# A state-space layer's sum over states: products with the unit matrix, or turned blocks added up in PSUM

## The chip, the core and the metric

The kernel runs on one core of a Trainium2 chip, in float32 throughout. The core's engines run side by side, each through its own queue in order: PE (TensorE, products, with its weight loads shown as PEld), DVE (VectorE), ACT (ScalarE, functions and copies), POOL (GpSimd) and SP, which here only issues DMAs. [...] The metric is the device time of one execution in microseconds, as the median of several runs; fewer is better.

## The reference, cut to what matters

Two transformer-like layers run over 4 sequences of 1024 tokens with 128 channels. Layer 0 is a selective state-space block (256 inner channels, 16 states) followed by a mixture of 8 experts and a shared one; layer 1 is a differential attention followed by routed attention and experts. The change lies in the state-space block:

```python
def step(h, inp):
    u_t, d_t, b_t, c_t = inp
    dA = jnp.exp(d_t[:, :, None] * A)
    h = dA * h + (d_t * u_t)[:, :, None] * b_t[:, None, :]
    y_t = jnp.einsum('bdn,bn->bd', h, c_t)      # the sum over the 16 states
    return (h, y_t)
...
y = ys.transpose(1, 0, 2) + uc * D
y = y * jax.nn.silu(z)
return y @ W_out.T
```

So for each channel and token, 16 products `h * c` are added up, `uc * D` is added, the result is gated by `silu(z)` and goes through the output product.

## The kernel before

**Tiling.** Layer 0 works on eight half-sequences of 512 tokens (`Half`, g = 0 to 7). Channels lie on the 128 partitions, in two groups (j = 0, 1), tokens along the free axis, so that one state of one channel group is a 128x512 tile.

**One state of one group** goes through four steps. `decay` (L446, ACT) makes the exponential `m_da`. `drive` (L450, POOL) makes `m_hb` = du * b, in one of seven buffers. `scan` (L458, DVE) runs the recurrence over the 512 tokens into the PSUM tile `m_hh`; in the first half of a sequence L462 keeps the last column as state, and L463 multiplies by c back into `m_hb`. `summed` (L466, PE) adds `m_hb` to the group's sum in PSUM, by a product with the unit matrix `ident` as weights and `m_hb` as the 512 moving columns. The two sums live in `banks[0]` and `banks[1]` (`d_x` in the profile), two PSUM tiles that all halves use in turn. A float32 product of 512 columns is two PE instructions with two weight loads in the profile.

**Around it.** `front` makes the inputs of a half (products L310, L318, L330, L345). `between` takes over after the last state: L368 (DVE) adds the sum bank to `uc * D`, L371 gates, L377 is the output product; then layer norm, the routing of tokens to experts and the turned input `f_xnT`. `Experts` runs nine experts for a half: `up` (L478, PE), `gelu` (L485, ACT), `down` (L500, PE) and `weighted` (L511 on DVE, L512 on POOL). Small PSUM results of `front`, `between`, `end` and `up` share four rotating banks (`bank()`, `l` in the profile); `f_yp` and `m_hh` have one bank each.

**Order.** Nothing is scheduled at run time. The string `ORDER` was written by a planner: each letter emits one step, and every engine's queue has its instructions in that order. For layer 0, `F` is a step of `front`, `f` fetches b and c of a state by two DMAs on SP, `a`, `r`, `s`, `y` are decay, drive, scan and summed, `B` and `E` are steps of `between` and `end`, and `u`, `g`, `d`, `w` are up, gelu, down and weighted. Halves overlap: while one half is scanned, PE and ACT run the experts of an earlier one. Exponentials and gelus use different function tables of ACT; each change from one to the other puts a table load (ACT_TABLE_LOAD) into ACT's queue.

In layer 1, the attention turns 128x128 blocks of its weights by PE (`nc.tensor.transpose`, L846) and copies them out of PSUM on ACT (L851).

Of the kernel before, what the change touches and what calls it, by code (L numbers as in the profile page):

```python
# [10 lines left out]
F32 = mybir.dt.float32  # L11
# [6 lines left out]
P = 128  # L18
# [28 lines left out]
def model_kernel(ctx: ExitStack, tc: tile.TileContext, a: dict, out: bass.AP):  # L47
# [100 lines left out]
    def normalized(dst, w, n, pool):  # L148
# [9 lines left out]

    TAKES = "GHIJKNOQ"
    ORDER = (  # L160
        "FFFFFFFFFFFFFFFFfFfFFFaFraFffFrsraafffaFafaaysaysrfyasrayasrrrryFFrssFyFayrrsFrrafrssaraFsFyfsyayysy"
        "fssFasaFayyaFFayfrFrysfrarsyrsyrsrrrsfyaFaaFsrfFyyssfyrrasrsayassryasaysaayayfrarsyfyyysaFrrssyfrFFB"
        "rBFaaBFsrfBrFsrFByFyFfBFrysfBsBaBBaayBrfuuuBrusBaBrFggfsguauyByaggaryaaasysrFsryrrsfBFdyudfgasyruruy"
        "wgggsuygfssasduaaarudrguryugfyuaysguyusgrFwfyrsauaagsrsrgdaydguFgfrdrufrywguysgraFsssayrgrryysfufugf"
        "usyuuagsgdryaaysruuayayusyswfaygdfadrargsyusuFgggBBBygaaaBayfrrraasruwdgrsgdBayFrsyFdywFsdBaruuFfrsf"
        "wsgBByyffBrsyruygdusFrBaasyffrgyrgsdauBauysayrasuBruadygswgdsrrugBgsuagrrysayFrfayFuBBuswagysgFysryg"
        "frusBayfaasuradFsaddswuayfsdarugugfugysrgugyFgufgFraursssayyrFsryryauaEgywuufdggadryaauEfssyagygEuru"
        "sggrBwruuFfrsugyrygarddasyudafgBrrwugyafBgudggFsysuBugrydudgsgwBBFugyuFBFwrFfgBrassudfsaraFsBFFfdwrg"
        "ysrsfrasuyaBBrFrugyagyauaaysayugdfrsysugydgausrrFawfyayBsarsFBFrudysFasrafauaygBdruFFyugfswysygsgrfy"
        "gBsFasBduurdsrafEyurudadFfyFsggwugEgwEyuudyFFrfgrsudafaaugwyguyasryyussyusdggggBaardBguaBuaauywrdudg"  # L170
        "fygBaufssuyadrBgfrsgurgwrFrusadBrsryagrgBFygrFuysBBuFgfrywsgugdBarryusffayBaafssssyararFyFrBsydurFug"
        "guBgyswgrauayBFfasyysyusaBFsdfuggByruradyuafrFsgggdusufyfdguraugasuywrdFgswdsFrgFuygrryrFaasfayruysa"
        "auragwFyusrydudgrgsFugafyfugursyFwugdgrduagyFsfsrausaayygfgdadwruursrBayfuyasgBFgagduwgaFsFadFgarasB"
        "ssufryyyrdrwauuysFguggBryasarsdauFBsygguwsFfusfgadsByydrrFyyfygsuysfyrsuarFsFEBrggyurdBFwfBgfarBfdyu"
        "usraaEfgsuadwsaEBafBusBdBryuygyrrrwrugugggyusagygBBFarrFdysuasduuauwygydsfgsfFuussFufurggrduurgaugyy"
        "dgauFfdwarasyuygsugyugsdyggaagygrusrwraaaudasuagggasBBrsyuawBsryrgfrBaBufrgrrrgFdsfayfrBFyuyadFuyasu"
        "frrdgggBfswusyFFFEsgugayduyBudsssawfyBEgsduygBasBrrdudrwfaufrsyuyuEgafFBuuasuryagguyggayaaFrggBgrrsd"
        "BarysrrawssysrdawyufgysyBFBgdFdusrwrsusayuyfudyuaFgdfrgrusggFuggfrwsduygFasagrdsuysayyuugggaaEadwysf"
        "uuyEuygsyrsgEduBawuuugBBggrgBddyfruaurBdggarwdauudgrufsgywuasyBrsgfrBruBygBgdBafufBsuggfduwysByaBugu"
        "gsugrdugasyuyrsBruaywagduggadrsyugrBsffruwragryrugaaausfraBagyyugdsrsrgsfuasuyryradsyusddagsuyswsguf"  # L180
        "gayudfsadgwgaurwugduggrsryguyayssryudurafyyuraggssywyayEygsgdayasrgyuEsuugrgysydBguBBwgduBEgduguBduw"
        "guBguggdudLSBBBSBdguuuwuggSdSSSwguSBguggduupBBpgppBugpgquuuBugqpBgdduqwpdgudwguggguuquwdpgdpgudqguwu"
        "ugqpduwguddwuggugugddugpugugdgdqwuguuduggEgqduggpgpwdEwqEdqwppqEEqppEqqRPMMXPMXMXcXPMcMCXXPMMcCXCTPX"
        "MMcXPXTMXTTMCXPTcMXTTMcPXMCCMTXTTPXcTMMVXPXccCMMCTXVTXPMTCXTcMCTPXMcVMCXTPMXTXcTMXTCPMXcMTXVPMTcXMCC"
        "TTXPMcTMVXTXPMMTCXcCpqTPXTMXcMVXTPTMcpXTqCMCXPTMXcMCVXPMTcpXMCTqPXMcMTXTXTPTCMcXpqTMXCPMTMcXVTPXCMMc"
        "TXVXPMcTCXTpMPpCqMMXXTqcXPCTMMXVTcPMXTMVXTcPCMXTCXMcTTPXMTMVXXcTcPMMCTCXVXTPTMXcMTpqPCMXCTXMVTPXMTcc"
        "XpqCMTXPTMMCXXVTPTMXcTMpCqPcMXTMXVTPXTCMcXMTXpPcMcMCqXTVPXMTMXpqCTcPMXTCXcCTTPCMXMXTMcpPCMqpXcMTVXTP"
        "MXcTCMXVTPXpTMcMXVTCXPMTTcCXTMTPXCMpXTcMXVPMcTXTMTCCPXMcMTXCXVTPTMXTTPcMXCMcTXMVPMXTXCcTTPMCXMXTMXVP"
        "TpcpMXMcCqPMqXTMXVCXTcPTMTMXpqcpPCXMcqVXTMTPCXTTppMMXcPCCqqXTMXcMCVTPMMXTcpCXqXpPqMXcVTTCMPXMTMXcTTC"
        "PXTMcMCXVTPXTMpXTcMCPqXMTcXCMVTPMXTcXMpTCqPMXTMcVXTPXMTCTXMpcTPCqMXcMTXVTPXMMCTXTpqcCXkPMcXVTTPMXMTM"  # L190
        "TcXpCCTPqMXcTXVMTPMMVCkXXXlkcPMXcCTpMPMqVkXXPMMlXcTMTcXkCCTlXPTTMXcTTCMXPTMklXCTMTXcPTMCMXVPkpcMXqMV"
        "XTTXCPcTMCTcXMpqTPkCXMclTXTMVXPTTMXpMckqlXCCPMcMTXXVTPMTpXMqklXPcMTXCMVCTPXMcTTpMcXXqklcPCMMTVCXXPTc"
        "TMCTpMkCXqPXlTMkkcXlMPlXTMXMXCVcTPMTMXVTCTPcXTMkMclXklXPTMTkXpPMlCCXcMCqMTXXVTPTccTMkXlMCpCPqXMTXMVT"
        "cTXPCTMMXcVXTPTCklpMMXcqTPCMXMTcXXVTPcTTMpMkCXqPXlCTMMcVXXTcPMTCTXklpMPMqMXTVcXCXTPTMTMkpXclPXMCMqCT"
        "XVTXPMTXcMklcXkPTlMMCcCXTCTPXTMMTkXlXkcPMcVMCVXTPXTMCXcMkTTXkPMMVcXXCTPTMcCCTXTPMMXkXkcMCTTPMXXMTcVk"
        "PMXcTCTMXTTXPMMXcVXpTpPMCTcXMVCXTPTTMMpXTcpPpCMCqXVqXTMTXcPTpMXMCqpcPMqCMXTXVTPXTMcMcpXpCPqqMMXTVXCX"
        "TcPTTMXppqCPMXcqTMcCMXCTXVPMTMXVTcCXPTMcMTXTpqXPTMCTXpcMTqXCPTMXcMVTPXTMTMXcCCpTPqXMcTMXkVPXTMpXMCcT"
        "PqCMXcTXMVTXPMMcTXCTCpPMqXcMTXVTPMXTCTMpXPkqMMcXXclkVPMCXTVXMTPkCXMXMcTlXPcMCTTMXkTPlXTcklMMCXcTCTPM"
        "XTTMCcXXVcPMkTCCXVMTTPXMTTcXTpMPqkMCXMcCplVXqXPMTTXklpMPcMqVXXMTCTPMcXTcTMXpkqCPlMXTMXVTCXPMTMXccpqk"
        "XPlCTMMXVTXcPCTpMkqlMcXTCTPMMXTCVXTXPcTMXcMCklklPXMCTTTMcVXTPXMCTMkXklPclMXTXMVTPCMXTpcXCMkPlqcMXTXM"  # L200
        "XVCTPTTckMXplMSPqCXTcMMCTVXPMXcTMVXTXPTMMTkCcXclTCXPTpqMMpkXSqXPMlCTTcXMCVPMXTcMcTkXpPlqXTTMMCcCVXSP"
        "MXkXclpPCMMCqXTTXTcTMPMkXlXTMkcPlXMMTVXXTCPTCMcMTcXCTkPlXkMXMVkkkTCTPXMkTcMXcTXTPMXCMVCTPMcXTMCTXXcV"
        "PCMMTTcXTPXkMTMXcVTCXPMTcCMXVTPMXTCcXMCTpXcTPMTMTXVPXMTpTpMpXCqTPpcMXMqVXCTPXTMccMXpqCpPMMqXXcCTVCXP"
        "TTMMpXqpqcPMXTMVXTCPMcCXMcCTTpXpqPMXMcqTTXCVPMXcMkTTCpXTPMqXTcMXCVXTPTMXMcpCTqPXTMcXMVTPCXMTcTXTTMPX"
        "CMcCTXMVTPMXcTXppqMCPMXcqCVMXTTXPTMTcpXTMCPqMXMTVXTPMcXcTXpPkMqMMXlVXCckTPXMCCTXMcVPkMkXllMcXCTTXPTM"
        "MkclXTTPXMCMTXTTCcPCMXTMTVcXPMMVkXXpCqcTPXMTTXpTPMqckMXlCXMVCXTPMTTpXqcklMPcMMXTXCVXTCTPcTMXpkMPqXlc"
        "MMCCTXVTXPTMpMXkqclXPMCMcTXVTPXTCTMcTCpXMkPclqXTMMXVcXTCTPTkMXMkcPllCMCXTVXTTMXPcTMMXXkcklPTClMMXCVT"
        "cXPMTcpkXPMqCXlTMMTXTCTPXMTMTpckXPClcMqMXcVVXPXTTkMMXClpPqcXMMCTVXTTPCXTTMcpcMkXqlPMXTMVCXTXCPTMcpCM"
        "XklcPMMqCXTXVTPXMccMTpkXqPlXCMMTTXTTCcPXMMkclXkTPClMXTCMXTcTPMkXlXkMXVPCcMVXTMXcCTPTMXcMVPXMMTCTcCXT"
        "XTPMTXMTXCcTPMTcCCXTMXPMcVXTTMPXkMTpMXXTPqCMcMTXVcppPMXpqXVCTTMPCXMXkcMTVPcMXMXTVCPXTCMTXcCTcMTPXCMT"  # L210
        "XcMCTXVPTTMXTMTXPcCMTcMVCXTPMXTTMXcXCTTcPMCMXVXVcCTTTTkkTTVkVZk00kGkklkGllk0lkkG0lklG01kGlkkllkklkll"
        "klk0lklGklklklklklkl0kGl0kGkk0k10kGk0YG20H302GIIG03HG202IIG2G50G2I00GG0G00GG0I02IG0GGJ2I0J2IG200G2GI"
        "10I00HG1G2G2I2I0IH0G420G7I22IGI0223IJ12IG210I2IH0GI0GGH22II0G240I21GHI22II20IG20GI0G120H2I12G1I0HI21"
        "1IGH23220I1GHIHI2JHI12KI21IH2KH1I36H113JH2H1J1HI2H11344HI1JK22H1HHK3J133JH11IJ3HIH1HJ3113H3H11HH31JJ"
        "JJ3133JHJ43J3J3KJ36H1JHJ11H34HKJ3J14HKO11H3H1O6HJ3J33J1JH313JHJ433OJK1341JKJ3J4H474K363KJ34HJJO345J3"
        "KKNK3JJ4N36K4J4OK463K4K4K3O4JKJ643OKK44KK643J5O6JKO644KNK654O4KK6O4K6644NK6OO44KOO6OK6O66OKO64OK656O"
        "NO454KK6O6O4NK64OK66O6O6O5N4OK4K6O456N4K5OK6O66NO5O556NN6N6Q5OOO6QO576N65Q7QOON67N7O5Q5N56ON5NN5Q6N5"
        "N5O7QN655NON75Q77NQ5N575N7Q5N6N5QN77Q55N75QQNQ7QN7Q577QQ77Q7Q7Q74QQ7NKQ5N57QN7Q7Q75QN75NQ7557Q7QN7NQ"
        "5Q57NQO7NQ74Q5N75Q77NQQ757Q7NQKQ7Q7Q"
    )  # L220
    f1 = tc.alloc_tile_pool(name="f1", bufs=1, side="right")
    f2 = tc.alloc_tile_pool(name="f2", bufs=2, side="right")
    ph = ExitStack()
# [18 lines left out]
    def bank(shape=None):  # L242
        return ps.tile(shape or [P, HALF], F32, name="l0")
# [25 lines left out]
    class Half:  # L269
# [93 lines left out]

        def between(self):

            y = self.uc
            for j in range(2):
                nc.vector.scalar_tensor_tensor(  # L368
                    y[:, j, :], y[:, j, :], vec[:, j, V_D : V_D + 1], banks[j], ALU.mult, ALU.add
                )  # L370
            nc.vector.tensor_tensor(y, y, self.zs, ALU.mult)  # L371
            yield
            yield
            po = bank([P, 4, C])
            for i in range(4):
# [87 lines left out]
            nc.vector.tensor_tensor(hb, hh, self.ct[n], ALU.mult)  # L463

        def summed(self, n, j):
            nc.tensor.matmul(banks[j], ident, self.hb[n, j], start=n == 0, stop=n == NS - 1)  # L466

    class Experts:

# [983 lines left out]
```

## Time and profile before

| | |
|---|---|
| median of 3 runs | 2672.36 us (2665.95 to 2677.88) |
| the profiled execution: its time, its span | 2661.41 us, 2659.6 us |
| granted TensorE clock, mean | 0.967 |
| PE, DVE, ACT, POOL busy, share of the span | 91%, 80%, 73%, 45% |
| sums, L466 | 512 PE instructions, first at 44.6 us, last at 859.9 us |
| experts' products, L478 and L500 | 576 PE instructions each |
| first product of layer 1's attention, L811 | at 965.6 us |

The whole span is a mean over stages with different limits. Layer 0 takes the first 965 us or so, the attention of layer 1 runs to about 2050 us, the rest is the routed layer. A stage is read best from busy times in stretches: an engine that is busy for all of a stretch sets its length, and an engine that idles for a few us only is close behind. Lengths of PE instructions overlap[...]; what one costs is the time from its start to the start of the next.

### The profile page before, as it was taken

The page shows a single profiled execution, that of the slowest core. Times are in us where ns is not written, and L with a number is a line of the kernel's source. Part 1 is how long each engine was busy: PE and PEld are TensorE (multiplying, and loading weights), DVE is VectorE, ACT ScalarE, POOL GpSimd, SP SyncE. Part 2 cuts the span into 40 slices and gives each one's busy share as a digit, 9 for nine tenths or more (in the row PEclk, how much of TensorE's full clock was granted, in tenths as well). Part 3 has the DMA queues.
Part 4 walks back from the last instruction along what each step waited for, and adds up shares of the span by engine and source line. Part 5 has one row for each costly group of instructions (what it writes and reads, how often), then busy time and mean ns, then how long its engine had stood idle before and what let it go on. Part 6 is the DMA issues. An engine that isn't in the chain of part 4 may idle for free.

```text
span 2659.6 us, 32447 instructions
## 1 busy us (share of the span) xinstructions
PE 2423.0 (91%) x10886; PEld 1182.7 (44%) x10886; DVE 2140.0 (80%) x4086; ACT 1949.9 (73%) x3058; POOL 1209.1 (45%) x619
## 2 busy tenths in 40 slices
PE   5699999999999978989998999899988889998987
PEld 2244444444444434445454545454544444444442
DVE  5988998898887448898889889988897776777656
ACT  5398889999998648889988998999896234332423
POOL 4868767867656125555556555654553000000000
PEclk8799999999999989999999999999999899999999
DMA  6323334433343411102110211021100000000000
GB/s 184 105 89 107 105 90 105 103 105 88 97 99 76 134 58 33 45 5 80 40 41 1 80 40 40 2 75 39 39 9 1 1 0 5 5 4 5 0 1 16
DMA packets 84010, 143.07 MB, mean 54 GB/s; under 512 B 11634, under 2 KB 27395, under 8 KB 83843
## 3 DMA queue, kind: packets, MB, share of 16 engines
q1 hardware_dynamic: 82722, 140.14, 18.8%
q8 instruction: 86, 1.41, 0.2%
q10 hardware_dynamic: 1120, 0.86, 0.1%
q14 instruction: 82, 0.66, 0.1%
HBM read 121.29 MB, written 19.66 MB: 53 GB/s over the span
## 4 chain that ended last, share of the span: by engine, by line
PE 63%; DVE 16%; ACT 14%; issue 3%; POOL 3%; DMA 0%; ACTq 0%; DVEq 0%; POOLq 0%
PE f_yp L500 8%; PE l L478 8%; PE d_sp L811 7%; PE r_a L1089 6%; PE d_x L466 6%; ACT d_pt L825 6%; DVE d_m L821 6%; PE d_x L860 5%; PE d_x L846 4%; PE r_a L1239 2%; ACT d_wT L851 2%; DVE m_hh L458 2%; DVE d_pt L839 2%; PE r_b L1216 2%; PE r_b L1067 1%
## 5 line engine op out<-in xcount | busy, mean ns | idle before, releaser
L821 DVE TENSOR_REDUCE d_m<-d_sp 128x1 f32<-128x1024 f32 x512 | 612.1, 1218 | 95.3 <-PE d_sp L811 93.6
L825 ACT ACTIVATE d_pt<-d_sp,d_m 128x1024 f32<-128x1024 f32 x512 | 574.7, 1123 | 54.5 <-DVE d_m L821 42.1
L450 POOL TENSOR_TENSOR m_hb<-m_du,m_bt 128x512 f32<-128x512 f32 x256 | 456.2, 1804 | 139.4 <-PE d_x L466 124.5
L836 POOL TENSOR_TENSOR d_pt<-d_pt,d_cf 128x1024 f32<-128x1024 f32 x128 | 263.4, 2058 | 474.7 <-DVE d_cf L831 385.9
L811 PE MATMUL d_sp<-d_k,d_q 32*128 32x512 f32 x2048 | 299.4, 652 | 56.5 <-ACT d_pt L825 54.3
L846 PE MATMUL d_x<-ident,d_pt 128*128 128x128 f32 x2048 | 316.3, 285 | 28.8 <-ACT d_wT L851 11.4
L846 PEld LDWEIGHTS d_x<-ident,d_pt 128*128 128x128 f32 x2048 | 219.8, 142 | 262.3 <-issue 94.4
L851 ACT COPY d_wT<-d_x 128x512 f32<-128x512 f32 x512 | 291.7, 591 | 60.8 <-PE d_x L846 57.9
L837 POOL TENSOR_TENSOR d_pt<-d_pt,d_pt 128x1024 f32<-128x1024 f32 x128 | 315.6, 2466 | 10.0
L466 PE MATMUL d_x<-m_hb,ident 128*128 128x512 f32 x512 | 266.0, 624 | 34.8 <-DVE m_hb L463 34.4
L478 PE MATMUL l<-f_xnT,w 128*128 128x512 f32 x576 | 281.6, 594 | 3.1 <-ACT f_ht L485 2.1
L500 PE MATMUL f_yp<-f_ht,w 128*128 128x512 f32 x576 | 274.2, 605 | 5.6 <-DVE f_cb L511 3.8
L860 PE MATMUL d_x<-d_wT,d_v 128*64 128x256 f32 x2048 | 249.0, 386 | 3.0 <-ACT d_wT L851 2.4
L485 ACT ACTIVATE f_ht<-l,b 128x512 f32<-128x512 f32 x288 | 185.3, 687 | 67.6 <-PE l L478 53.8
L446 ACT ACTIVATE m_da<-m_delta,neg_a 128x512 f32<-128x512 f32 x256 | 171.7, 714 | 38.1 <-DVE m_hh L458 32.4
L512 POOL TENSOR_TENSOR f_acc<-f_acc,f_cb 128x512 f32<-128x512 f32 x64 | 115.1, 1799 | 163.8 <-DVE f_cb L511 163.7
L458 DVE TENSOR_TENSOR_SCAN m_hh<-m_da,m_state,m_hb 128x512 f32<-128x512 f32 x128 | 175.6, 1372 | 16.4 <-ACT m_da L446 3.7
L463 DVE TENSOR_TENSOR m_hb<-m_hh,m_ct 128x512 f32<-128x512 f32 x256 | 176.0, 688 | 7.5
L458 DVE TENSOR_TENSOR_SCAN m_hh<-m_da,m_hb 128x512 f32<-128x512 f32 x128 | 169.7, 1326 | 13.0 <-POOL m_hb L450 1.7
L860 PEld LDWEIGHTS d_x<-d_wT,d_v 128*64 128x64 f32 x2048 | 136.2, 137 | 94.6 <-issue 18.9
L466 PEld LDWEIGHTS d_x<-m_hb,ident 128*128 128x128 f32 x512 | 98.0, 199 | 171.7 <-issue 96.8
L500 PEld LDWEIGHTS f_yp<-f_ht,w 128*128 128x128 f32 x576 | 108.6, 192 | 145.8 <-issue 129.0
(277 smaller groups left out, 3599.9 us busy)
## 6 DMA issues: line engine op xcount, KB each, us to landing
m_bt<-m_bcd SPq DMA_DIRECT2D x128, 256.0 KB
m_ct<-m_bcd SPq DMA_DIRECT2D x128, 256.0 KB
f_cb<-f_cbd SPq DMA_DIRECT2D x64, 256.0 KB
d_q<-d_qf SPq DMA_DIRECT2D x128, 128.0 KB
d_qf<-d_qks SPq DMA_DIRECT2D x16, 512.0 KB
d_kf<-d_qks SPq DMA_DIRECT2D x16, 512.0 KB
d_k<-d_kf SPq DMA_DIRECT2D x128, 64.0 KB
x<-in_x_dram SPq DMA_DIRECT2D x4, 512.0 KB
```

Of the source, the lines that this page charges most:

```text
L450: nc.gpsimd.tensor_tensor(self.hb[n, j], self.du[:, j, :], self.bt[n], ALU.mult)
L458: nc.vector.tensor_tensor_scan(hh, self.da[n, j], hb, 0.0 if self.h == 0 else state[:, j, n : n + 1], ALU.mult, ALU.add)
L466: nc.tensor.matmul(banks[j], ident, self.hb[n, j], start=n == 0, stop=n == NS - 1)
L478: nc.tensor.matmul(self.hp[i], w1[:, e, k * P : (k + 1) * P], self.half.fT, start=True, stop=True)
L500: nc.tensor.matmul(self.yp[e][0], w2[:, e, k, :], ht[:, k % 2, :], start=k == 0 and e < E, stop=k == NK - 1)
L811: nc.tensor.matmul(self.sp[s][:, c * HALF : (c + 1) * HALF], q[g, self.qb * P : (self.qb + 1) * P], k[g, :], start=True, stop=True,)
L821: nc.vector.tensor_reduce(self.m[s], self.sp[s], AX.X, ALU.max, negate=True)
L825: nc.scalar.activation(pt, self.sp[s], AF.Exp, bias=self.m[s], accum_out=self.se[:, s : s + 1])
L837: nc.gpsimd.tensor_tensor(p, p, p_2, ALU.add)
L846: nc.tensor.transpose(tp[:, i, :], self.pe[0][:, kb * P : (kb + 1) * P], ident)
L851: nc.scalar.copy(wTs[key][:, :, a, qi * P : (qi + 1) * P], tp)
L860: nc.tensor.matmul(op[a * 64 : (a + 1) * 64, :], self.batch.v[hp][:, c * 4 + i, a * 64 : (a + 1) * 64], wTs[self.n // (2 * QG), c][:, i, a ...
```

## The change

`summed` no longer multiplies by the unit matrix. Each 128x512 tile `m_hb` is taken as four 128x128 blocks; each block is loaded as weights, the unit matrix moves through as 128 columns, and PE works in its mode for turning (`is_transpose`). The turned blocks are added to what the bank holds, so at the end a bank holds the sum with tokens on the partitions and channels along the free axis, block by block.

`between` has to turn it back: two copies on ACT bring the banks into SBUF (`yt`, in the two buffers of `f_xn`), eight plain turns on PE put them into two of the four rotating banks (`yp`), and the multiply-and-add of L368 reads those instead of the sum banks. This adds steps, so `B` stands 144 times in `ORDER` instead of 128 times, and the planner wrote a new `ORDER` for the whole kernel. Its other letters are as many as before.

```diff
     ORDER = (
-        "FFFFFFFFFFFFFFFFfFfFFFaFraFffFrsraafffaFafaaysaysrfyasrayasrrrryFFrssFyFayrrsFrrafrssaraFsFyfsyayysy"
+        "FFFFFFFFFFFFFFFFfFFFFFarFraafsfarfasfsfyrfyraaaarfaassfrraFsafyrysraarrssyyaaaFrsarssysFfyryaFyfrFfy"
...
         def between(self):
 
             y = self.uc
+            yt = [f2.tile([P, 4, C], F32, name="f_xn") for _ in range(2)]
             for j in range(2):
+                nc.scalar.copy(yt[j], banks[j].rearrange("p (n c) -> p n c", c=C))
+            yield
+            for j in range(2):
+                yp = bank()
+                for i in range(4):
+                    nc.tensor.transpose(yp[:, i * P : (i + 1) * P], yt[j][:, i, :], ident)
+                yield
                 nc.vector.scalar_tensor_tensor(
-                    y[:, j, :], y[:, j, :], vec[:, j, V_D : V_D + 1], banks[j], ALU.mult, ALU.add
+                    y[:, j, :], y[:, j, :], vec[:, j, V_D : V_D + 1], yp, ALU.mult, ALU.add
                 )
             nc.vector.tensor_tensor(y, y, self.zs, ALU.mult)
-            yield
             yield
...
         def summed(self, n, j):
-            nc.tensor.matmul(banks[j], ident, self.hb[n, j], start=n == 0, stop=n == NS - 1)
+
+            for i in range(4):
+                nc.tensor.matmul(
+                    banks[j][:, i * P : (i + 1) * P],
+                    self.hb[n, j][:, i * P : (i + 1) * P],
+                    ident,
+                    is_transpose=True,
+                    start=n == 0 and i == 0,
+                    stop=n == NS - 1,
+                    skip_group_check=True,
+                )
```

## The prediction

> **What bounds the kernel now.** First the page's busy times, then the first layer cut at the first scan of each of its eight half-sequences (columns: busy us and instructions of PE, PEld, DVE, ACT, POOL; granted clock; DMA share; GB/s):
>
> ```profile
> PE 2423.0 (91%) x10886; PEld 1182.7 (44%) x10886; DVE 2140.0 (80%) x4086; ACT 1949.9 (73%) x3058; POOL 1209.1 (45%) x619
> ...
> 41.50:124.80 83.30, 51.60 (x79) 15.52 (x79) 76.01 (x125) 40.37 (x55) 79.95 (x40) 0.75 0.38 106
> 124.80:219.10 94.30, 89.61 (x216) 38.69 (x216) 83.75 (x113) 83.12 (x104) 65.11 (x34) 0.94 0.32 96
> 219.10:317.80 98.70, 94.80 (x241) 42.12 (x241) 89.20 (x158) 84.97 (x108) 79.22 (x42) 0.98 0.38 108
> 317.80:430.10 112.30, 109.50 (x282) 49.14 (x281) 102.14 (x165) 95.30 (x120) 78.60 (x45) 0.98 0.34 93
> 430.10:535.10 105.00, 104.11 (x264) 46.33 (x263) 94.85 (x175) 99.80 (x121) 79.91 (x44) 1.00 0.39 104
> 535.10:640.10 105.00, 104.65 (x271) 47.13 (x270) 94.72 (x132) 100.02 (x124) 75.77 (x43) 0.98 0.36 99
> 640.10:750.70 110.60, 110.60 (x288) 50.18 (x287) 95.29 (x173) 101.67 (x126) 74.54 (x44) 1.00 0.39 100
> 750.70:858.20 107.50, 106.47 (x275) 48.46 (x274) 86.00 (x129) 99.58 (x121) 65.82 (x39) 1.00 0.37 87
> 858.20:965.60 107.40, 104.35 (x302) 49.72 (x300) 43.16 (x156) 57.06 (x83) 17.36 (x14) 1.00 0.39 110
> ```
>
> From half 1 on PE is the limit, 95 to 100% busy. But ACT is right behind: from half 4 on it idles 5.2, 5.0, 8.9 and 7.9 us. Half 0 is DVE's. The last row is the tail after the last scan, again PE's. A busy PE need not be at its peak, so I take PE's cost from starts, in the timeline (start, length):
>
> ```profile
> 310.84 1.02 PE L478 MATMUL l<-f_xnT,w 128*128 128x512 f32 x2
> 311.69 0.60 PE L429 MATMUL l<-ident,f_acc 128*128 128x128 f32 x4
> 312.13 1.02 PE L466 MATMUL d_x<-m_hb,ident 128*128 128x512 f32 x2
> 312.99 1.88 PE L478 MATMUL l<-f_xnT,w 128*128 128x512 f32 x4
> ```
>
> A product of 512 columns (two instructions) holds the queue from 312.13 to 312.99, 0.86 us; four turned blocks from 311.69 to 312.13, 0.44 us. Last, what DVE and ACT wait for between 60 and 860 us, and the groups that price the rest:
>
> ```profile
> DVE f_cb L511 <- PE f_yp L500: 20.0, 9, 5.0
> DVE o_st L250 <- PE l L377: 9.9, 5, 4.0
> ...
> ACT f_ht L485 <- PE l L478: 19.9, 25, 2.2
> ```
> ```profile
> L846 PE MATMUL d_x<-ident,d_pt 128*128 128x128 f32 x2048 | 316.3, 285 | 28.8 <-ACT d_wT L851 11.4 <-POOL d_pt L837 8.5 <-ACT r_lnc L792 2.0
> L851 ACT COPY d_wT<-d_x 128x512 f32<-128x512 f32 x512 | 291.7, 591 | 60.8 <-PE d_x L846 57.9
> L485 ACT ACT_TABLE_LOAD x100 | 128.3, 1283 | 2.1 <-PE l L478 0.3
> L446 ACT ACT_TABLE_LOAD x99 | 127.0, 1283 | 2.6 <-DVE m_hh L458 0.9
> ```
>
> DVE's waits in that stretch add up to 57 us, 33 of them for PE. Its idle time there is about 93 us; the other 36 us are steps of under 0.2 us between its own instructions, some 5 us a half, which nobody ends earlier.
>
> **The change part by part.**
>
> The sums (L466): 256 products at 0.86 become 256 groups of four turned blocks at 0.44: 256 x 0.42 = 107.5 us off PE.
>
> Turning back in `between`: 16 groups of four plain turns, 16 x 0.44 = +7.0 us on PE. PE's net is -100.5 us, about 12.5 a half in the steady part.
>
> [...] The group of plain turns at L846 has 285 ns for one. [...] But 285 ns is how long one is shown, not how far apart they start: the timeline has 0.11 us a block, and I use that. As for the clock: between 985 and 2050 us, where L846 turns 2048 blocks, 512 groups at 0.44 to 0.59 us (a quarter of the time), the granted clock is 0.99. In the new first layer turns take 32 x 0.44 = 14 us of a half's 105. I put no clock loss.
>
> Adding to what is in PSUM with a turned block is not in the trace. Ends: 0.44 us a group, as plain turns; or 0.89, if such a block costs as an ordinary product of 128 columns (L377: 16 instructions, two a block, in 1.78 us), which puts PE at 256 x 0.03 + 7 = +15 us. [...] I take 0.44: the same kind of instruction, and ordinary products that add (L478 starts afresh, L500 adds) step alike.
>
> Copies out of the two sum banks: 16 on ACT by L851's row, 16 x 0.591 = +9.5 us. Table loads: the built order of ACT has 250 in the first layer against 256, -6 x 1.283 = -7.7 us. ACT's net is +1.8 us, but not evenly spread: up to the first decay of half 7 it is about +8, after it -6. DVE is unchanged: the 16 L368 instructions read a PSUM bank before and after. POOL and SP have the same instructions and DMAs, in almost the same place against the scans; nothing of theirs is moved past a queue.
>
> The new wait: the copies stand in ACT's queue between gelus and decays, and each waits for the last of a half's sums. Behind it are the gelus that free PSUM banks for `up`, and the next half's first sum waits for the copy as it waited for L368. I take nothing for it: in the order 1 to 5 scans of the next half stand ahead of that first sum (2 to 4 before), at 1.35 + 0.69 us each, and seven m_hb buffers let scans go on. Without that cover it costs up to a few us a half (rival C).
>
> **The sum.** PE's 100 us can't all be had: what a half can shrink is set by the next engine. Half 0: DVE idles 7.3, less 5 of steps: 2 us. Halves 1 to 3: DVE's 10.6, 9.5, 10.2 less 5 each: 15 us (ACT has more). Halves 4 to 7: ACT's 5.2, 5.0, 8.9, 7.9 less some 1.3 of steps each: 22 us (DVE has as much or more). The ceiling is 39 us, 37 with ACT's 1.8. How much of it comes? As long as PE leads, it runs at 99%; in the second layer's attention (985 to 2050), where PE, DVE and ACT are near each other, PE is busy 971.7, DVE 935.2 and ACT 948.3 of 1065, so the fullest still idles 9%. After the change the first layer looks more like that. I take half: -18 us.
>
> The tail: the order puts 45 `up` and 27 `down` behind the last scan (44 and 27 before), so PE-bound work of about 107 us stays; the chain of copy, turn and L368 is longer by 1.2 + 0.9 us, beside leftover products of half 6. +1 us. The second layer's instructions are the same, with some neighbours swapped: 0, a few us either way.
>
> So -17 us on the profiled execution's own time, 2661.4 to 2644.4. It was 11 us below the median of the three runs (2672.36); I carry the difference over: 2655 us, -0.65%.
>
> **Rivals.**
>
> A, the forecast (0.52): ACT and DVE become the limit and return about half the ceiling. For: ACT at 95% in halves 4 and 5 already. Gain 10 to 28 us: 2644 to 2662.
>
> B (0.16): PE was what broke the others' flow, the ceiling is returned whole and shorter waits let the neighbours move too. For: 33 of DVE's 57 us of waits name PE, and gelu waits 19.9 us for L478. Against: the attention stage shows no engine reaching 97%. 37 to 46 us: about 2630.
>
> C (0.12), slower: the handing-over of the sum banks. The copy stands in the fullest queue; a late copy holds the next half's first sum, then m_hb fills, POOL's L450 stops (it waited 124.5 us for L466 in all before) and DVE's scans with it. Each handing-over that stalls 5 us costs 7 x 5 = 35 against the gain of 17: +18, about 2690. It decides from 2.5 us each on. Against: L368 stood in a queue nearly as full, and waited 2.2 us in all. The dear end of the adding turns (+15) lands at the same place.
>
> D (0.20): ACT is already the limit in disguise: its extra 8 us before half 7 eat what the halves from 4 on could give, and only halves 1 to 3 gain. 0 to 10 us: 2662 to 2672.
>
> **How the numbers follow.** A difference of 0.5% (13 us) is about what measurement can tell from none; the three runs span 12 us. Faster by more: all of B and 0.75 of A, 0.55. Slower by more: C and a little noise, 0.13. Within: 0.32. The range reaches from B's end, 2626, to C's weaker form, 2684.
>
> **What would show it.** Right: sums' groups step 0.44 us; PE's busy share in halves 4 to 7 drops to about 90%; ACT's rises to 97% or more; halves 4 to 7 last 102 to 106 us; the first attention product (965.6 us before) starts near 949; second layer unchanged. Wrong: groups of 0.8 us or more (adding turns are dear); ACT idle before or behind the copies, and POOL's waits for the sums growing (C); a granted clock under 0.95 in these halves; halves of under 100 us (B: ACT wasn't a floor).

## The result, and the profile after

The changed kernel takes 2645.99 us in the median (2645.25 to 2647.33), against 2675.12 us for the kernel before beside it (2665.95 to 2677.94): a ratio of 0.990 (0.987 to 0.992), 1.0% faster. Its profiled execution took 2645.31 us, with a span of 2643.5 us, 16.1 us less than the span before. The medians differ by 29 us and the traces by 16, since the traced execution of before (2661.41 us) lies at the fast end of that kernel's runs; what a longer one of them spends its time on was not traced. Line numbers have moved: `decay` is L453, `drive` L457, the scan L465, the multiply by c L470, the sum L475, `up` L495, `gelu` L502, `down` L517; in `between` the copies are L369, the turns L374, the multiply-and-add L376, the output product L384.

The busy times of the page, and the first layer cut at the first scan of each half and at the first attention product, as before (columns: busy us and instructions of PE, PEld, DVE, ACT, POOL; granted clock; DMA share; GB/s):

```profile
PE 2346.8 (89%) x11462; PEld 1213.8 (46%) x11462; DVE 2143.2 (81%) x4086; ACT 1950.2 (74%) x3068; POOL 1208.3 (46%) x619
```
```profile
42.10:126.40 84.30, 41.83 (x151) 26.66 (x152) 76.93 (x125) 44.43 (x58) 78.97 (x41) 0.62 0.37 104
126.40:222.60 96.20, 82.08 (x288) 44.35 (x289) 86.06 (x114) 82.75 (x103) 65.34 (x36) 0.91 0.31 99
222.60:326.00 103.40, 89.34 (x313) 46.19 (x312) 90.90 (x157) 96.18 (x118) 73.33 (x42) 0.92 0.32 99
326.00:437.20 111.20, 98.81 (x349) 51.14 (x347) 102.01 (x164) 99.78 (x125) 71.72 (x44) 0.95 0.32 98
437.20:543.00 105.80, 96.25 (x340) 48.97 (x339) 93.37 (x175) 97.26 (x123) 83.10 (x45) 0.98 0.32 98
543.00:641.20 98.20, 96.21 (x347) 49.44 (x346) 90.15 (x133) 95.48 (x122) 75.10 (x41) 1.00 0.38 106
641.20:743.60 102.40, 97.45 (x362) 51.18 (x361) 93.79 (x166) 97.04 (x122) 78.02 (x43) 1.00 0.36 106
743.60:839.50 95.90, 92.50 (x342) 49.01 (x341) 88.13 (x129) 89.38 (x114) 73.34 (x41) 1.00 0.32 99
839.50:948.80 109.30, 104.82 (x308) 50.87 (x306) 45.57 (x162) 59.23 (x87) 17.37 (x14) 0.99 0.40 119
```

Halves 0 to 4 together became 7 us longer (500.9 us against 493.6), halves 5 to 7 became 27 us shorter (296.5 against 323.1), the tail 2 us longer. The first attention product starts at 948.8 us instead of 965.6. From there to the end of the span it is 1694.7 us against 1694.0: the second layer is unchanged. (In the traces of all experiments this part takes 1693.8 to 1702.4 us, so a few us between two single executions say little.)

The adding turned blocks, on PE in the timeline (start, length):

```profile
567.32 0.60 PE L475 MATMUL d_x<-ident,m_hb 128*128 128x128 f32 x4
567.76 1.88 PE L517 MATMUL f_yp<-f_ht,w 128*128 128x512 f32 x4
569.48 1.04 PE L475 MATMUL d_x<-ident,m_hb 128*128 128x128 f32 x8
570.35 1.88 PE L517 MATMUL f_yp<-f_ht,w 128*128 128x512 f32 x4
```

A group of four holds PE's queue for 0.44 us, two groups for 0.87 us. The waits between 60 and 840 us (total us, times, longest), and the groups of the sums, the scans and the multiply:

```profile
DVE f_cb L528 <- PE f_yp L517: 12.2, 6, 4.5
...
DVE m_uc L376 <- PE l L374: 1.1, 2, 0.9
...
ACT f_ht L502 <- PE l L495: 8.1, 15, 1.9
...
POOL m_hb L457 <- PE d_x L475: 142.2, 80, 7.7
POOL f_acc L529 <- DVE f_cb L528: 43.8, 27, 9.1
```
```profile
L475 PE MATMUL d_x<-ident,m_hb 128*128 128x128 f32 x1024 | 158.2, 292 | 53.3 <-DVE m_hb L470 51.5 <-ACT f_xn L369 1.8
L465 DVE TENSOR_TENSOR_SCAN m_hh<-m_da,m_state,m_hb 128x512 f32<-128x512 f32 x128 | 176.5, 1379 | 10.1
L470 DVE TENSOR_TENSOR m_hb<-m_hh,m_ct 128x512 f32<-128x512 f32 x256 | 176.0, 687 | 7.0
L465 DVE TENSOR_TENSOR_SCAN m_hh<-m_da,m_hb 128x512 f32<-128x512 f32 x128 | 169.7, 1326 | 13.9 <-POOL m_hb L457 2.1 <-issue 1.3
```

The handing-over is cheap: PE waited 1.8 us in all for the copies, and DVE 1.1 us for the plain turns. DVE's waits for `down` fell from 20.0 to 12.2 us, ACT's for `up` from 19.9 to 8.1 us. POOL's waits for the sums grew from 124.5 to 142.2 us.

**What sets the pace.** The chain of work that ended last, followed back through halves 1 to 7, by line (share of that stretch; the profile prints the longest entries and stops at its width; "issue" is time in which an engine waited for nothing that the profile shows), before and after:

```profile
by line: PE f_yp L500 24.0%; PE l L478 22.5%; PE d_x L466 20.9%; PE l L310 3.8%; ACT m_da L446 3.0%; ACT L446 2.6%; ACT f_ht L485 2.6%; DVE m_hh L458 2.3%; ACT L485 2.2%; PE l L377 1.8%; POOL m_hb L450 1.3%; PE l L330 1.3%; PE l L318 1.2%; 
```
```profile
by line: PE f_yp L517 13.5%; PE l L495 13.2%; DVE m_hh L465 12.5%; PE d_x L475 6.3%; DVE m_hb L470 5.2%; ACT m_da L453 4.7%; issue 4.5%; ACT f_ht L502 4.4%; ACT L502 4.0%; ACT L453 3.8%; DMA f_cb<-f_cbd 1.8%; DVE f_ln L258 1.7%; PE l L345 1
```

Of the entries shown, PE's make up 75.5% before and 33% after; DVE's go from 2 to 19%, ACT's from 10 to 17%. After the change the chain passes from one engine to the next.

**Work that moved.** The new order also moves work between halves. ACT's busy time is 4 us more in half 0, 13 more in halves 1 to 4 and 19 less in halves 5 to 7. Most of it is table loads of `decay` and `gelu`: 13 fewer in halves 5 to 7 (17 us), first before, then after, and 11 more in halves 2 and 3.

```profile
L485 ACT ACT_TABLE_LOAD x47 | 60.3, 1283 | 0.8
L446 ACT ACT_TABLE_LOAD x45 | 57.7, 1283 | 0.8
```
```profile
L502 ACT ACT_TABLE_LOAD x40 | 51.3, 1283 | 0.7
L453 ACT ACT_TABLE_LOAD x39 | 50.0, 1283 | 0.7
```

**Where PE's relief went.** In halves 1 to 7 PE is busy for 652.6 us instead of 719.7, 67 us less, but it idles 60.5 us instead of 13.7. So 47 of 67 came back as idle time, and 20 us were won. In halves 1 to 3 the granted clock fell as well: 0.91, 0.92 and 0.95, against 0.94, 0.98 and 0.98. One place shows how such a hole comes about. This is the timeline of all engines in half 2:

```profile
270.62 2.67 POOL L457 TENSOR_TENSOR m_hb<-m_du,m_bt 128x512 f32<-128x512 f32 x2 [0.23 <-PE d_x L475]
...
270.70 1.46 DVE L142 TENSOR_TENSOR t_eq<-t_eq,before 128x256 f32<-128x256 f32 x1
...
271.23 0.60 PE L475 MATMUL d_x<-ident,m_hb 128*128 128x128 f32 x4
...
275.04 1.23 DVE L465 TENSOR_TENSOR_SCAN m_hh<-m_da,m_hb 128x512 f32<-128x512 f32 x1
...
277.11 1.12 PE L475 MATMUL d_x<-ident,m_hb 128*128 128x128 f32 x4 [5.28 <-DVE m_hb L470]
...
283.73 1.06 PE L475 MATMUL d_x<-ident,m_hb 128*128 128x128 f32 x4
...
284.58 1.91 PE L495 MATMUL l<-f_xnT,w 128*128 128x512 f32 x2
```

And the same place in windows of 8 us (columns as above):

```profile
262.40:270.40 8.00, 8.00 (x32) 3.89 (x31) 7.76 (x12) 7.83 (x12) 6.03 (x4) 1.00 0.38 111
270.40:278.40 8.00, 2.72 (x13) 1.62 (x12) 7.57 (x14) 5.98 (x8) 2.73 (x3) 0.73 0.16 61
278.40:286.40 8.00, 8.00 (x13) 3.08 (x14) 6.85 (x12) 5.66 (x7) 3.31 (x2) 0.50 0.36 123
286.40:294.40 8.00, 8.00 (x27) 3.88 (x26) 3.95 (x7) 7.94 (x12) 7.74 (x4) 0.91 0.09 33
```

DVE ranks the tokens for the experts (L140 to L154) from 268.6 to 275.0 us and gives no new `m_hb`. Three of these instructions (L141 to L143) take 1.49, 1.46 and 1.37 us with POOL's `drive` beside them; the median of L142 is 0.42. PE, whose queue has the next sum at its head, runs dry for 5.28 us, up to 277.11 us. In windows of 1 us the granted clock is 1.00 up to 274 us, 0.50 from 275 to 287 us and 1.00 again from 288 us, some ten us after PE resumed; a group takes 0.85 us (283.73 to 284.58), about twice its 0.44. The same happens near 400 us in half 3: 4.92 us idle up to 404.77 us, and a granted clock of 0.50 from 404 to 414 us. Before, PE never idled for over 2.2 us between the first scan of half 1 and the last scan. That the longer products filled those holes is likely, but the order differs too. What brings the clock down was not shown: it was also 0.50 from 258 to 260 us, where PE's gaps just before were 1.93 us (up to 254.05 us) and 1.54 us (up to 256.68 us).

### The profile page after: what moved, and what is told of

Read it like the earlier page. It is cut to its first block, busy times and chain, and to the rows that moved or that the text cites. A ratio compares the mean times of both kernels' runs of the same rounds, so it can differ in the third digit from the quotient of the medians.

```text
span 2643.5 us, 33657 instructions
## 1 busy us (share of the span) xinstructions
PE 2346.8 (89%) x11462; PEld 1213.8 (46%) x11462; DVE 2143.2 (81%) x4086; ACT 1950.2 (74%) x3068; POOL 1208.3 (46%) x619
## 4 chain that ended last, share of the span: by engine, by line
PE 52%; DVE 22%; ACT 17%; issue 5%; POOL 4%; DMA 1%; SPq 0%; ACTq 0%; DVEq 0%; POOLq 0%
PE d_sp L828 7%; PE r_a L1106 6%; ACT d_pt L842 6%; DVE d_m L838 6%; PE d_x L877 5%; PE f_yp L517 5%; PE l L495 5%; PE d_x L863 4%; DVE m_hh L465 4%; ACT d_wT L868 2%; PE r_a L1256 2%; DVE d_pt L856 2%; PE r_b L1233 2%; PE d_x L475 2%; DVE m_hb L470 2%
## 5 line engine op out<-in xcount | busy, mean ns | idle before, releaser
L457 POOL TENSOR_TENSOR m_hb<-m_du,m_bt 128x512 f32<-128x512 f32 x256 | 449.6, 1775 | 150.6 <-PE d_x L475 142.2
L495 PE MATMUL l<-f_xnT,w 128*128 128x512 f32 x576 | 288.3, 609 | 16.4 <-ACT f_ht L502 9.5
L517 PE MATMUL f_yp<-f_ht,w 128*128 128x512 f32 x576 | 271.0, 600 | 8.1 <-DVE f_cb L528 5.3
L502 ACT ACTIVATE f_ht<-l,b 128x512 f32<-128x512 f32 x288 | 185.0, 687 | 43.7 <-PE l L495 27.1
L475 PE MATMUL d_x<-ident,m_hb 128*128 128x128 f32 x1024 | 158.2, 292 | 53.3 <-DVE m_hb L470 51.5
L475 PEld LDWEIGHTS d_x<-ident,m_hb 128*128 128x128 f32 x1024 | 130.8, 150 | 146.7 <-issue 71.6
L453 ACT ACTIVATE m_da<-m_delta,neg_a 128x512 f32<-128x512 f32 x256 | 171.3, 715 | 34.6 <-DVE m_hh L465 29.6
L465 DVE TENSOR_TENSOR_SCAN m_hh<-m_da,m_state,m_hb 128x512 f32<-128x512 f32 x128 | 176.5, 1379 | 10.1
L470 DVE TENSOR_TENSOR m_hb<-m_hh,m_ct 128x512 f32<-128x512 f32 x256 | 176.0, 687 | 7.0
L465 DVE TENSOR_TENSOR_SCAN m_hh<-m_da,m_hb 128x512 f32<-128x512 f32 x128 | 169.7, 1326 | 13.9 <-POOL m_hb L457 2.1
L529 POOL TENSOR_TENSOR f_acc<-f_acc,f_cb 128x512 f32<-128x512 f32 x64 | 119.1, 1861 | 134.6 <-DVE f_cb L528 121.9
L877 PEld LDWEIGHTS d_x<-d_wT,d_v 128*64 128x64 f32 x2048 | 136.2, 137 | 94.8 <-issue 18.6
L856 DVE SCALAR_TENSOR_TENSOR d_pt<-d_pt,d_cf,d_pt 128x1024 f32<-128x1024 f32 x128 | 167.3, 1307 | 2.9 <-DVE d_cf L848 0.5
```

Source lines behind the costliest of these rows:

```text
L457: nc.gpsimd.tensor_tensor(self.hb[n, j], self.du[:, j, :], self.bt[n], ALU.mult)
L465: nc.vector.tensor_tensor_scan(hh, self.da[n, j], hb, 0.0 if self.h == 0 else state[:, j, n : n + 1], ALU.mult, ALU.add)
L475: nc.tensor.matmul(banks[j][:, i * P : (i + 1) * P], self.hb[n, j][:, i * P : (i + 1) * P], ident, is_transpose=True, start=n == 0 and i == 0,
L495: nc.tensor.matmul(self.hp[i], w1[:, e, k * P : (k + 1) * P], self.half.fT, start=True, stop=True)
L517: nc.tensor.matmul(self.yp[e][0], w2[:, e, k, :], ht[:, k % 2, :], start=k == 0 and e < E, stop=k == NK - 1)
L877: nc.tensor.matmul(op[a * 64 : (a + 1) * 64, :], self.batch.v[hp][:, c * 4 + i, a * 64 : (a + 1) * 64], wTs[self.n // (2 * QG), c][:, i, a ...
```

## The experiments

Theory 1 in the expectations is the forecast's: once PE is lighter, DVE's and ACT's busy time are the floor of the first layer. Theory 4, made after the first four runs, has no engine as the floor: they wait for one another in turn. Ratios are to runs of the kernel before made beside each, with the 95% interval; the changed kernel's is 0.990 (0.987 to 0.992), and its span 2643.5 us.

### One table for ACT, before and after

In both kernels the experts' gelu in layer 0 becomes Identity, so their values are other ones, and ACT needs some 172 and 165 fewer table loads: about 220 us off ACT.

```diff
-            nc.scalar.activation(self.ht[i // 2][:, k % 2, :], self.hp.pop(i), AF.Gelu, bias=b1[:, j : j + 1])
+            nc.scalar.activation(self.ht[i // 2][:, k % 2, :], self.hp.pop(i), AF.Identity, bias=b1[:, j : j + 1])
```

> The kernel before, with the gelu of the experts in layer 0 replaced by the identity with the same bias, so that exponentials and gelus share a function table and some 170 table loads (about 220 us of ACT) go; the experts' values are other ones. Theory 1 (the limit was PE, and ACT and DVE took over after the change): layer 0 stays PE-bound, at most 10 us faster than before, halves 4 to 7 still 103 to 110 us. Theory 2 (neither: the written order and its waits set the pace in both kernels): also next to nothing. Theory 3 (ACT was already level with PE): 20 us or more.

> The same replacement in the changed kernel (gelu of layer 0's experts as identity, other values, some 165 table loads less). Theory 1: ACT's part of the floor goes and DVE's stays, so up to DVE's idle time beyond its steps in halves 1 to 7 (68.6 - 35 = 33 us) can come: 10 to 30 us faster than the changed kernel, 2616 to 2636 us. Theory 2 (the written order's waits set the pace): within 8 us of it. Theory 3 (DVE alone is the floor): within 5 us, with DVE's idle time unchanged.

On the kernel before: 2657.47 us, 0.995 (0.993 to 0.997), first attention product at 960.6 us. That is some 14 us by the ratio, above the 10 that theory 1 allowed: ACT's work was worth something even beside a full PE. On the changed kernel: 2651.86 us, 0.992 (0.990 to 0.994), span 2645.0 us, against 2643.5 with all table loads. ACT now idles 28 to 48 us in each half from 1 on, and the time does not get shorter. ACT alone was no floor there, and this part of theory 1 fell.

### Half of the multiply by c, before and after

The multiply covers 256 of the 512 columns; the other half of the sum's input stays du * b.

```diff
-            nc.vector.tensor_tensor(hb, hh, self.ct[n], ALU.mult)
+            nc.vector.tensor_tensor(hb[:, 0:256], hh[:, 0:256], self.ct[n][:, 0:256], ALU.mult)
```

> The kernel before, with the multiplication by c (L463) on 256 of its 512 columns: 256 x about 0.33 = 85 us of DVE less, the other half of the products is left out. Theory 1: half 0, where DVE is the limit, becomes up to 10 us shorter; from half 1 on PE holds: 10 to 15 us faster than before in all. Theory 2: about 10 us, half 0 alone. Theory 3 (DVE level with PE): 30 us or more.

> The changed kernel with the multiplication by c on 256 of 512 columns (85 us of DVE less). Theory 1: half 0 up to 10 us shorter, and of the later halves those where DVE was the fuller one; ACT's idle time in halves 1 to 7 (55 us, some 10 of steps) is the ceiling: 20 to 40 us faster than the changed kernel, 2606 to 2626 us. Theory 2: half 0 alone, about 10 us. Theory 3 (DVE alone is the floor): 50 us or more.

On the kernel before: 2661.78 us, 0.996 (0.995 to 0.998), some 11 us, as theory 1 had it; but not where it had it, since half 0 became only 0.8 us shorter. On the changed kernel: 2644.8 us, 0.991 (0.988 to 0.994), span 2640.6 us: again nothing. The groups of the changed kernel with half the multiply:

```profile
L465 DVE TENSOR_TENSOR_SCAN m_hh<-m_da,m_state,m_hb 128x512 f32<-128x512 f32 x128 | 196.9, 1539 | 10.1
L465 DVE TENSOR_TENSOR_SCAN m_hh<-m_da,m_hb 128x512 f32<-128x512 f32 x128 | 187.6, 1466 | 15.3 <-POOL m_hb L457 3.5 <-ACT m_da L453 1.0 <-DVE m_hb L470 0.5
L470 DVE TENSOR_TENSOR m_hb<-m_hh,m_ct 128x256 f32<-128x256 f32 x256 | 107.6, 420 | 7.0
```

The multiply gave up 68 us (176.0 to 107.6), and the untouched scans took 38 us more (346.2 to 384.5). With other instructions that took longer too, DVE's busy time on the page fell by only 21 us (2143.2 to 2122.6), so this is a weaker test of DVE than it was meant to be.

### Both together

> The changed kernel with both reliefs at once: gelu of layer 0's experts as identity (no change of function table) and the multiplication by c on 256 of 512 columns; values are left out and other ones. Each alone gave nothing. Theory 4 (after the change PE, DVE and ACT take turns on the chain that sets the end, so that freeing one leaves the other two): with two freed, PE alone is left at some 90 us a half; halves 1 to 4 (416 us in the changed kernel) shrink by 25 us or more, halves 5 to 7, where PE's queue is full already, by under 10: 2600 to 2620 us. Theory 2 (the written order makes engines wait for one another whatever their load): within 10 us of the changed kernel.

2625.39 us, 0.982 (0.981 to 0.984): about 20 us faster than the changed kernel, where each edit alone gave none. Halves 5 and 6 of it:

```profile
528.00:623.20 95.20, 95.15 (x347) 49.71 (x346) 86.32 (x133) 70.63 (x104) 73.46 (x41) 1.00 0.40 109
623.20:720.10 96.90, 95.98 (x359) 50.90 (x358) 89.96 (x165) 66.18 (x98) 79.89 (x43) 1.00 0.39 111
```

With both neighbours lighter PE is busy 95.15 of 95.20 us: it leads again. In halves 1 to 4 the gain was 14 us and in 5 to 7 11 us. Theory 4 had 25 or more and under 10, theory 2 10 at most in all; both missed. What holds: in the changed kernel neither PE nor ACT nor DVE alone sets a half's length; the chain passes from one to the next, and taking one link's work away leaves the others.

### Old operations in the new order

`between` stays as before, with two empty steps so that the new `ORDER` fits (the diff is against the kernel before).

```diff
     ORDER = (
-        "FFFFFFFFFFFFFFFFfFfFFFaFraFffFrsraafffaFafaaysaysrfyasrayasrrrryFFrssFyFayrrsFrrafrssaraFsFyfsyayysy"
+        "FFFFFFFFFFFFFFFFfFFFFFarFraafsfarfasfsfyrfyraaaarfaassfrraFsafyrysraarrssyyaaaFrsarssysFfyryaFyfrFfy"
...
+            yield
+            yield
```

> The old operations (products with the unit matrix, the sum banks read by DVE) in the changed kernel's order. If the gain comes from the turned blocks: no gain, PE full again, 2665 to 2690 us. If the new order brought it: 2645 to 2655 us.

2696.0 us, 1.009 (1.007 to 1.011): the new order with the old products is slower, and by more than expected. So the order by itself is no improvement, and the gain needs the turned blocks.

### The new operations in the old order

First with all of the handing-over in the one old step, the turned blocks going back into the sum banks. Against the changed kernel, beside the old `ORDER` and the steps that go with it:

```diff
-                yp = bank()
                 for i in range(4):
-                    nc.tensor.transpose(yp[:, i * P : (i + 1) * P], yt[j][:, i, :], ident)
-                yield
+                    nc.tensor.transpose(banks[j][:, i * P : (i + 1) * P], yt[j][:, i, :], ident)
...
-                    y[:, j, :], y[:, j, :], vec[:, j, V_D : V_D + 1], yp, ALU.mult, ALU.add
+                    y[:, j, :], y[:, j, :], vec[:, j, V_D : V_D + 1], banks[j], ALU.mult, ALU.add
```

> The new operations in the old order: turned blocks in the sums; copies, turning back (into the sum banks themselves) and multiply-and-add stand together where the multiply-and-add stood, so DVE's queue waits there for copy and turn, about 2 us for each of 16. PE is 100 us lighter all the same. Theory 4: half of the changed kernel's gain or more, 2650 to 2665 us. If the planner's new order is what made the gain: 2670 us or more.

2687.18 us, 1.006 (1.004 to 1.009). Then with the handing-over as in the changed kernel, and two more `B` put into the old order behind the first of each half, so that copy, turns and multiply-and-add stand apart (the first place is shown):

```diff
-        "rBFaaBFsrfBrFsrFByFyFfBFrysfBsBaBBaayBrfuuuBrusBaBrFggfsguauyByaggaryaaasysrFsryrrsfBFdyudfgasyruruy"
+        "rBBFaBaBFsrfBrFsrFByFyFfBFrysfBsBaBBaayBrfuuuBrusBaBrFggfsguauyByaggaryaaasysrFsryrrsfBFdyudfgasyrur"
```

> The changed kernel's operations in the old order, this time spread as in the changed kernel: copies where the multiply-and-add stood, the two turning-back groups and multiply-and-adds in the four slots behind it, two of them new, two and four letters later. The first try had them all in one slot and DVE waited 26 us there. If that stand-in alone spoiled it: 2645 to 2662 us, DVE waiting under 8 us for the turned-back sums. If the new operations only pay with an order written for them: 2665 us or more.

2701.97 us, 1.013 (1.010 to 1.015). Both are slower than the kernel before, though PE has 100 us less to do. DVE's wait for the turns, in the first and in the second:

```profile
DVE m_uc L373 <- PE d_x L372: 21.6, 5, 10.6
```
```profile
DVE m_uc L376 <- PE l L374: 27.2, 6, 9.5
```

It was 1.1 us in the changed kernel. Rival C's stall is real where the order leaves no room for the copy and the turns; the new order has the room. The two `B` were put in by hand: this is the old order with the new steps added, and not an order planned for them.

### Less PE work, nothing added

On the changed kernel, two of four turned blocks are left out for all states but the first and the last, some 49 us of PE:

```diff
-            for i in range(4):
+            for i in range(4 if n in (0, NS - 1) else 2):
```

> The changed kernel with two of the four turned blocks left out of every sum but the first and last state's: 224 x 0.22 = 49 us of PE less, otherwise the same. Theory 1 (PE has given up the limit): within 5 us of the changed kernel. Theory 4: halves 5 to 7, where PE's queue is 93 to 96% full by steps, get 2 to 5 us shorter each, halves 1 to 4 hardly: 5 to 15 us faster. If PE is still the limit: 25 us or more.

2649.75 us, 0.992 (0.991 to 0.994), span 2651.3 us: no gain. On the kernel before, the products of the same states run over 256 of 512 columns, some 96 us of PE, which is about the relief that the change brings:

```diff
-            nc.tensor.matmul(banks[j], ident, self.hb[n, j], start=n == 0, stop=n == NS - 1)
+            m = HALF if n in (0, NS - 1) else HALF // 2
+            nc.tensor.matmul(banks[j][:, 0:m], ident, self.hb[n, j][:, 0:m], start=n == 0, stop=n == NS - 1)
```

> The kernel before in its own order, with 256 instead of 512 columns in the sums of all but the first and last state: 224 x 0.43 = 96 us of PE less, about what the change takes off PE net, and nothing added; half of the sums is left out. If PE's relief is worth something by itself: 15 to 37 us faster than before (37 is the ceiling of DVE's and ACT's idle time). If an order written for a full PE can't use a lighter one: under 10 us. The difference to the kernel with all new operations in this order is what copies, turning back and handing-over of the banks cost.

2669.21 us, 0.9995 (0.998 to 1.001): nothing. Halves 2 to 4 of it:

```profile
218.00:322.40 104.40, 91.26 (x240) 43.67 (x239) 95.30 (x157) 85.75 (x110) 76.88 (x42) 0.93 0.35 100
322.40:436.80 114.40, 105.98 (x287) 50.91 (x285) 103.14 (x164) 92.36 (x117) 78.68 (x45) 0.94 0.34 91
436.80:544.40 107.60, 95.75 (x262) 46.24 (x263) 100.79 (x175) 99.83 (x124) 80.18 (x44) 0.97 0.35 101
```

PE idles 8 to 13 us in each, where it idled 1 to 4, and the clock is 0.93 to 0.97 instead of 0.98 to 1.00. Its sums are still ordinary products, so a lower clock came with the idle stretches without the turning mode. And DVE needs longer for the same instructions: 95.3 us for 157 in half 2, where the kernel before needed 89.2 for 158, and 2158.4 us against 2140.0 on the page (one execution of each).

### POOL's part

POOL makes `m_hb` for 256 columns and clears the rest, so it multiplies half as much:

```diff
-            nc.gpsimd.tensor_tensor(self.hb[n, j], self.du[:, j, :], self.bt[n], ALU.mult)
+            nc.gpsimd.memset(self.hb[n, j][:, 256:HALF], 0.0)
+            nc.gpsimd.tensor_tensor(self.hb[n, j][:, 0:256], self.du[:, j, 0:256], self.bt[n][:, 0:256], ALU.mult)
```

> The changed kernel with POOL's drive on 256 of 512 columns, the other 256 set to zero by a memset (which reads nothing); half of the driving terms is left out. Freed PE, ACT or DVE alone gave nothing. If POOL's work beside DVE's scans is the hidden limit: POOL's 449.6 us and the scans' 346 us both fall (the scans towards 256 x 1.23 = 315), and layer 0 gets 20 us or more shorter. If the scans' wait and POOL's just follow from who stands where: 10 us or less, and POOL waits the more for the sums.

2635.7 us, 0.987 (0.986 to 0.989), span 2628.0 us. Against the changed kernel that is 10 us less in the median, but 6 by the ratios, whose intervals overlap; the traced execution is the fastest of its four, 15 us below that of the changed kernel. So a gain is likely and its size open. In the trace all of it lies in halves 1 to 4 (402 us instead of 417; halves 5 to 7 take 296 in both).

```profile
L458 POOL TENSOR_TENSOR m_hb<-m_du,m_bt 128x256 f32<-128x256 f32 x256 | 254.3, 993 | 13.5 <-DVE m_du L361 8.0 <-DMA m_bt<-m_bcd 5.5
...
L457 POOL MEMSET m_hb<- 128x256 f32 x256 | 79.5, 310 | 220.3 <-PE d_x L476 149.4 <-issue 52.9 <-DVE m_state L470 4.9
```

POOL still waits 149 us for the sums, so it has time left. The scans did not get shorter (352.6 us against 346.2), yet DVE's busy time on the page fell by 8.5 us, to 2134.7. So DVE's other instructions took some 15 us less beside the shorter `drive` (one execution of each).

Last, one more buffer for `m_hb`, with every queue in the same order, so that POOL waits less for the sums:

```diff
-            self.hb[n, j] = m3.tile([P, HALF], F32, name="m_hb", bufs=7)
+            self.hb[n, j] = m3.tile([P, HALF], F32, name="m_hb", bufs=8)
```

> The changed kernel with eight m_hb buffers instead of seven, nothing else[...]. POOL waits 142 us for the sums to release a buffer. If a tight coupling through these buffers costs time: 4 to 15 us faster than the changed kernel. If queue order sets the pace: within 3 us, with POOL's wait moved elsewhere.

2665.58 us, 0.997 (0.996 to 0.998), span 2660.1 us: this gives most of the gain away, which neither branch of the expectation had. POOL's waits between 60 and 840 us:

```profile
POOL f_acc L529 <- DVE f_cb L528: 94.8, 31, 11.3
POOL m_hb L457 <- PE d_x L475: 74.4, 38, 8.6
POOL m_ro L354 <- ACT m_ex L351: 21.2, 5, 10.1
```

The wait for the sums halved (142.2 to 74.4), and the wait for the weighted outputs doubled (43.8 to 94.8): POOL runs ahead and then stands before the next thing. But DVE's busy time on the page rose by 16 us to 2159.2, about as much as the span rose: the same instructions in the same order took longer while POOL ran more freely.

No kernel that computes all of the reference beat the changed one.

## Why the prediction was right or wrong

**The total.** Forecast: 17 us off the profiled execution, 2644.4 us. Measured: 16.1, at 2645.31 us. The median was forecast 9 us too high, at 2655, because I carried the 11 us between the profiled run and the median of before over to the changed kernel. There they aren't: its four runs lie within 2.1 us of each other, and the profiled one is among them. With four runs of before beside them the medians differ by 29 us. Direction and size held; several of the steps did not, and that the total fits so well is luck.

**Steps that held.** The adding turned block costs what a plain one does, 0.44 us for four. So the dear end (0.89) is out. PE's busy time fell by 76 us for the forecast's 100. By the estimate below, some 14 of the missing 24 are the slower clock: 10 in halves 1 to 7, 4 in half 0 and the tail. The rest was not traced. ACT's busy time rose by 0.3 us (forecast 1.8), the tail grew by 2 (1), the first attention product starts at 948.8 us (949), and the second layer is the same. No clock loss shows with the turning mode: halves 5 to 7 are granted 1.00 with 32 groups of adding turns in each.

**The step that failed: the ceiling.** I took what a half can shrink from the idle time of DVE and ACT, and half of it for what comes. The halves say otherwise: 1 to 4 became 6 us longer instead of some 9 us shorter, and 5 to 7 gave 27 us where their whole ceiling was 18. Half 5 lasts 98.2 us and half 7 95.9, below the 102 to 106 that I gave. In halves 4 to 7 PE's busy share is 91, 98, 95 and 96%, not about 90, and ACT's 92, 97, 95 and 93%, not 97 or more: PE did not hand the limit over to ACT. What I had wrong was ACT's load. I summed its change to +8 us up to half 7; that held, but by halves it is +17 in halves 0 to 4 and -9 in 5 and 6, and another -10 in half 7. The floor that I took from the old order was not there in the new one, and counting the table loads by halves in the new `ORDER` could have shown it beforehand. An idle time in one order is no floor for another. Freeing ACT alone (the one-table run) and lightening DVE alone gave nothing, and both together 20 us. The total came out because two misses cancelled. Half 0 was misread as well: its row has POOL at 79.95 of 83.30 us, above DVE's 76.01, and on the kernel before half of the multiply took 0.8 us off it.

**The step that I took for granted: PE's relief.** "From half 1 on PE is the limit, 95 to 100% busy" was right as a reading, and wrong as a price. Taking 96 us off PE in the old order gave 0.9995, while ACT's relief in the same order gave 0.995 and DVE's 0.996. A PE that is busy 99% beside DVE and ACT at 80 to 95% is one of three; behind it stands the chain that the trace of the changed kernel shows, through DVE's scans and ACT's exponentials and gelus. All four corners of the change were run:

| | old order | new order |
|---|---|---|
| products with `ident` | 1 | 1.009 (1.007 to 1.011) |
| turned blocks | 1.006 to 1.013 (two ways of handing over) | 0.990 (0.987 to 0.992) |

Each half of the change by itself is a loss. The gain belongs to the pair: the operations, and the order that was written with them.

**"I put no clock loss."** Right for the turns (1.00 in halves 5 to 7), wrong for the idle stretches that came with a lighter PE (0.91, 0.92 and 0.95 in halves 1 to 3). An estimate from the windows by half, PE's busy time times one minus the granted clock, summed over halves 1 to 7:

| kernel | PE's work less by, us | lost to the clock, us | ratio |
|---|---|---|---|
| before | 0 | 12 | 1 |
| after | 100 | 21 | 0.990 |
| after, half of `drive` | 100 | 11 | 0.987 |
| new order, products | 0 | 13 | 1.009 |
| after, one table and half multiply | 100 | 20 | 0.982 |
| before, half products | 96 | 29 | 0.9995 |
| after, one table | 100 | 26 | 0.992 |
| after, half multiply | 100 | 27 | 0.991 |
| after, eight buffers | 100 | 30 | 0.997 |
| old order, one step | 100 | 35 | 1.006 |
| after, half of the turns | 149 | 39 | 0.992 |
| old order, spread | 100 | 40 | 1.013 |

So about 10 us of the change's relief went back this way, in halves 1 to 3 (half 4's loss and half 5's gain cancel), and leaving out half of the turns gave back 17 of its 49. Once PE is no longer the one that leads, its work is worth less than its microseconds. The table does not show a cause: the old products in the new order lose little to the clock and are slow, and an idle PE and a low clock are also what a stall from elsewhere looks like.

**The rivals.** C did not happen (1.8 and 1.1 us of waits for the handing-over), though one of its signs came: POOL's waits for the sums grew from 124.5 to 142.2 us. C is what the old order would have brought: 21.6 and 27.2 us. B's sign, halves under 100 us, came in halves 5 and 7. D is out: halves 5 to 7 gained most. A's mechanism fell although its number held.

**What stays open.** Why halves 5 to 7 gained and 1 to 4 did not. In halves 5 to 7 the old products in the new order keep PE busy for 320 us, and the turned blocks in the old order keep ACT busy for 306 us; both are more than the 296.5 us that the changed kernel takes there in all. So neither half of the change could have gained that much alone. But those kernels take 322 and 332 to 336 us there, and whether ACT's lighter load is what let PE's relief pay was not tested: turned blocks in the old order with one table for ACT were not run. For halves 1 to 4 the run with half of `drive` points to POOL and DVE, no more. The trace has DVE's L142 at 1.46 and 1.38 us beside POOL and at 0.42 us without it (last section), and the run with a freer POOL, where DVE's same instructions take 16 us longer, goes the way that this would have it; that it is the cause was not shown. Untested is also the planner's part: one order was written for each kernel, and the orders and operations tried here lie between 0.990 and 1.013, so another order for the old products might have gained as much.

## What to carry to other kernels

Before you price a change by the engine that is busy 99%, take as much of its work away in the old order and look: here 96 us were worth nothing. In a kernel whose queues are in a planned order, an operation and the order around it are one change, so plan the order anew for the new operations, judge only the pair, and count each engine's work by stage in the new order before you price it. And where a lighter PE starts to wait, look at the granted clock beside its idle time: here a hole of 5.28 us came with a clock of 0.50 that lasted until some ten us after PE resumed.

## What the runs showed of the hardware

- While PE was without work for 5.28 us, up to 277.11 us, the granted clock fell from 1.00 to 0.50. It stayed 0.50 from 275 to 287 us, some ten us after PE resumed, and a group stepped 0.85 us instead of 0.44.
- With the multiply behind it cut from 687 to 420 ns, the scans went from 1379 and 1326 to 1539 and 1466 ns (one execution of each). 38 of the 68 us came back so.
- DVE's L142, over 128x256, runs eight times in layer 0 of the changed kernel: 1.46 us at 270.70 us and 1.38 us at 398.22 us, both beside POOL's work (`drive` from 270.62 us; `drive` from 397.76 and L529 from 399.28 us), and 0.42 to 0.43 us in the other six, with POOL idle. The cause was not shown.
- One more buffer cost time here: eight instead of seven for `m_hb`, with every queue in the same order, took 0.7% more time (0.997 against 0.990).
- A 128x128 float32 block turned and added to PSUM takes 0.109 us of PE's queue (0.87 us for eight), though one is shown as 292 ns long.
